# Relational messages on two row halves of the array, and the edge network's stores on ScalarE's DMA queue with a third input buffer

## The chip, the cores and the metric

The kernel runs on one core of a Trainium2 chip. The metric is the device time of one execution in microseconds. Before the change three timed executions took 13,983.0, 14,011.58 and 14,035.43 us, a median of 14,011.58. Engines are named as in the profile: PE does matrix multiplications (PEld its weight loads), DVE is VectorE, ACT is ScalarE, POOL is GpSimd, SP is SyncE, which here only issues DMAs.

## The reference

A graph with 3125 nodes of 64 features goes through four layers, each ahead of a layer norm and a relu. 100,000 edges, sorted by target, carry attributes of 32, 64 and 9 numbers and one of 65 relation types. Cut to the two places that the change touches:

```python
# layer 1 (tensor field): weights of every edge from its 64 attributes, once for k, once for v
def mlp2(x, w1, b1, w2, b2):
    return jax.nn.relu(x @ w1 + b1) @ w2 + b2
wk = mlp2(edge_features, k_w1, k_b1, k_w2, k_b2)      # [E, 128]
wv = mlp2(edge_features, v_w1, v_b1, v_w2, v_b2)      # [E, 128]
k = tensor_product(x_dst, edge_sh, wk, Cqk)           # sh: 9 numbers of every edge
v = tensor_product(x_dst, edge_sh, wv, Cv)

# layer 3 (relational convolution), twice: W_r is [65, 64, 64]
seg = dst * r + edge_type
msg = x[src]
agg = segment_sum(msg, seg).reshape(n, r, d)
cnt = segment_sum(ones, seg).reshape(n, r, 1)
mean = agg / maximum(cnt, 1.0)
out = einsum('nrd,rdk->nk', mean, W_r) + x @ W_root + b
# around it
conv = relu(out)
res = relu(h @ res_W[l] + res_b[l])
h = conv + res
```

Layer 0 is three transformer convolutions (attention over the incoming edges of a node), layer 2 two mean convolutions.

## The kernel before

The stages run one after the other: sorting the edges by target, three transformer loops, the tensor field's loop, two mean convolutions, two relational convolutions. Each loop goes over the edges in 49 groups; a group has 16 slots of 128 edges, and for every slot POOL issues one indirect DMA (`gather`, L56) that fetches 128 rows of a node table by index. Plain DMAs go through the helper `dma` (L53), which issues all of them on SP's queue, in the order in which SP reaches them: an instruction of SP that waits holds back all behind it. The engines each work through their own instructions in order; which order that is is decided by a scheduler at build time, apart from the few instructions marked `keep_in_program_order`.

*Relational convolution* (`rgcn`). The kernel multiplies first and gathers afterwards: for each of 25 blocks of 125 nodes it computes the product of the block with all 65 relation matrices, 125 x 4160 numbers, and stores them in the DRAM table `xw` (`store_nodes`). `edge_sum` then gathers one 64-wide row for each edge by source and relation. `hT` holds the transposed features (64 partitions; `transposed`, L340 and L341, over a PSUM tile `ptr` in two buffers), `wr` the 65 matrices side by side on the same 64 partitions. One block is one matmul for root and residual weights (L924, `po`, 128 columns), with two additions of biases on DVE (L925 and L926), and nine matmuls L931 into the PSUM tile `pm` (three buffers of one bank): eight of 512 columns (eight relations), and one of 64. Each `pm` is copied to `xs` (three buffers), by DVE (L936) and ACT (L934) in turn. Contraction runs over 64 partitions, so the matmuls use rows 0 to 63 of the array. In the profile every float32 matmul appears as two weight loads and two matmul records.

*Edge network* (`edge_weights`). A generator with 98 steps, each for eight slots of 128 edges, that the transformer loops draw on: two half steps in each third group, one half step in the other groups, so two steps to every three groups. A step loads `ef` (the 64 edge features and the nine harmonics, two buffers), transposes it over `pe` and `eT`, multiplies by the first weights (L565, the halves of the array in turn) with a relu on ACT into `hid` (L566), then splits the harmonics into three bf16 parts (L571 to L575) and transposes them into `sT` (L580), which two DMAs store in `sht`. Last it multiplies by the second weights (biases L588, products L594, PSUM tiles `pw`), and ACT copies the result into `wo` (L597); a DMA of 1024 KB stores it in `wt`. A further DMA writes zeros to `qxf`. ACT also does the transformer's own exponentials (L418, `ew`) in the same queue; DVE's L423 needs them and gives buffers free for later gathers.

Of the kernel before, what the change touches and what calls it, by code (L numbers as in the profile page):

```python
# [8 lines left out]
F32 = mybir.dt.float32  # L9
# [8 lines left out]
P = 128  # L18
N = 3125
NP = 125  # L20
NT = 25
D = 64
# [10 lines left out]
DE, DS, DF = 32, 9, 64  # L33
# [3 lines left out]
R = 65  # L37
# [4 lines left out]
def gnn_stack(ctx: ExitStack, tc: tile.TileContext, a: dict, out: bass.AP):  # L42
    nc = tc.nc
    V, S, PE, GP = nc.vector, nc.scalar, nc.tensor, nc.gpsimd
# [7 lines left out]
    def dma(dst, src):  # L52
        return nc.sync.dma_start(dst, src)  # L53
# [51 lines left out]
    wt = dram.tile([EP, 2 * OV], F32, name="wt")  # L105
# [4 lines left out]
    with tc.tile_pool(name="skey", bufs=1) as kp, tc.tile_pool(name="swork", bufs=2) as wp, tc.tile_pool(  # L110
        name="srow", bufs=3
# [11 lines left out]
        for name, pad in (("dst", N), ("src", 0), ("edge_type_65", 0)):  # L123
            t = kp.tile([P, NG, G], I32, name=f"k_{name}")
# [30 lines left out]
        for g in range(NG):  # L155
            oh = one_hots(g)
            for j in range(G):
                PE.matmul(ph, lhsT=oh[:, j, :HI], rhs=oh[:, j, HI:], start=(g == 0 and j == 0),
                          stop=(g == NG - 1 and j == G - 1))
# [4 lines left out]
        po = pp.tile([HI, 2], F32, name="po", tag="ph")  # L164
# [11 lines left out]
        for g in range(NG):  # L176
# [21 lines left out]
            for j in range(G):  # L198
                for s0, s1 in ((0, G // 2), (G // 2, G)):
                    s0 = max(s0, j)  # L200
# [320 lines left out]
    def edge_weights(cp, ep, pp):  # L521

        w1 = cp.tile([P, P], F32, name="w1")
        b1 = cp.tile([P, 1], F32, name="b1")
        w2 = cp.tile([P, OV], F32, name="w2")
        b2 = cp.tile([3, 2, OV], F32, name="b2")
        for i, nm in enumerate(("k", "v")):
            for k in range(2):
                dma(w1[k * D:(k + 1) * D, i * D:(i + 1) * D], a[f"L1_gnn_{nm}_w1"])
            dma(b1[i * D:(i + 1) * D, :], a[f"L1_gnn_{nm}_b1"].rearrange("(d o) -> d o", o=1))  # L530
            dma(w2[i * D:(i + 1) * D, :], a[f"L1_gnn_{nm}_w2"])
            dma(b2[:, i, :], bcast_rows(a[f"L1_gnn_{nm}_b2"], 3))

        parts = [cp.tile([3, 2, OV], BF16, name=f"b2p{k}") for k in range(3)]
        acc = cp.tile([3, 2, OV], F32, name="b2acc")
        for k, t in enumerate(parts):
            V.tensor_copy(t, b2)
            if k < 2:
                V.tensor_sub(b2, b2, t)
        V.tensor_scalar(acc, parts[0], ident[:3, 0:1], None, op0=ALU.mult)  # L540
        for k in (1, 2):
            V.scalar_tensor_tensor(acc, parts[k], ident[:3, k:k + 1], acc, op0=ALU.mult, op1=ALU.add)
        b2r = cp.tile([3, 2, OV], BF16, name="b2r")
        V.tensor_copy(b2r, acc)
        one3 = cp.tile([3, P], BF16, name="one3")
        V.memset(one3, 1.0)
        zeros = cp.tile([P, 8, OV], F32, name="zeros")
        V.memset(zeros, 0.0)
        rows = sht.rearrange("t k p -> (t k) p")
        for s0 in range(0, NS, 8):  # L550
            ef = ep.tile([P, 8, DF + DS], F32, name="ef")
            dma(ef, tab.rearrange("(p j) f -> p j f", p=P)[:, s0:s0 + 8, C64:C64 + DF + DS])
            pe = pp.tile([P, 4, P], F32, name="pe", tag="pe", bufs=2)
            for i in range(4):
                e2 = ep.tile([P, 2, DF], F32, name="e2")
                c = S.copy(e2, ef[:, 2 * i:2 * i + 2, :DF])
                if i == 0:
                    tc.keep_in_program_order(c)
                PE.transpose(pe[:, i, :], e2.rearrange("p a f -> p (a f)"), ident)
            eT = ep.tile([P, 4, P], F32, name="eT")  # L560
            S.copy(eT, pe)
            hid = ep.tile([P, 2, 4, P], F32, name="hid")
            for k in range(2):
                ph = pp.tile([P, 4, P], F32, name="ph", tag="pe", bufs=2)
                PE.matmul(ph, lhsT=w1[k * D:(k + 1) * D, :], rhs=eT[k * D:(k + 1) * D], start=True, stop=True)  # L565
                S.activation(hid[:, k], ph, AF.Relu, bias=b1)  # L566
            yield
            sh = ef[:, :, DF:]
            s3 = ep.tile([P, 8, 3, DS], BF16, name="s3")
            rest = ep.tile([P, 2, 8, DS], F32, name="srest")  # L570
            tc.keep_in_program_order(S.copy(s3[:, :, 0, :], sh))  # L571
            V.tensor_sub(rest[:, 0], sh, s3[:, :, 0, :])
            S.copy(s3[:, :, 1, :], rest[:, 0])
            V.tensor_sub(rest[:, 1], rest[:, 0], s3[:, :, 1, :])
            S.copy(s3[:, :, 2, :], rest[:, 1])  # L575
            pst = pp.tile([4 * 3 * DS, 2, P], BF16, name="pst", tag="pe", bufs=2)
            for q in range(2):
                PE.transpose(pst[:, q, :], s3[:, 4 * q:4 * q + 4].rearrange("p j k s -> p (j k s)"), identb)
            sT = ep.tile([4 * 3 * DS, 2, P], BF16, name="sT")
            S.copy(sT, pst)  # L580
            for q in range(2):
                t0 = (s0 + 4 * q) * 3 * DS
                dma(rows[t0:t0 + 4 * 3 * DS, :], sT[:, q, :])
            wo = ep.tile([P, 8, 2 * OV], F32, name="wo")
            for i0 in (0, 2):
                pw = [pp.tile([P, 2, 2, OV], F32, name=f"pw{m}") for m in range(2)]
                for m in range(2):
                    PE.matmul(pw[m], lhsT=one3, rhs=b2r[:, m, :].unsqueeze(1).to_broadcast([3, 4, OV]),  # L588
                              start=True, stop=False)
                for i in range(2):  # L590
                    for k in range(2):
                        for m in range(2):
                            r = slice(m * D, (m + 1) * D)
                            PE.matmul(pw[m][:, i, k, :], lhsT=hid[r, k, i0 + i, :], rhs=w2[r, :], start=False,  # L594
                                      stop=(i == 1 and k == 1))
                for m in range(2):
                    S.copy(wo[:, 2 * i0:2 * i0 + 4, m * OV:(m + 1) * OV], pw[m].rearrange("p i k o -> p (i k) o"))  # L597
            dma(wt.rearrange("(p j) f -> p j f", p=P)[:, s0:s0 + 8, :], wo)
            dma(qxf[0:EP, :].rearrange("(p j) f -> p j f", p=P)[:, s0:s0 + 8, :], zeros)
            yield  # L600

# [305 lines left out]
    def rgcn(l):  # L907
        xw = dram.tile([N, R * D], F32, name=f"xw{l}")
        with tc.tile_pool(name="rg", bufs=1) as fp, tc.tile_pool(name="rgp", bufs=2, space=PSUM) as pp:
            own = fp.tile([NP, NT, D], F32, name="own")  # L910
            res = fp.tile([NP, NT, D], F32, name="res")
            with tc.tile_pool(name="rw", bufs=1) as rp:
                wr = rp.tile([D, R, D], F32, name="wr")
                dma(wr, a["L3_gnn_W"][l].rearrange("r d k -> d r k"))
                wo = rp.tile([D, 2 * D], F32, name="wo")
                dma(wo[:, :D], a["L3_gnn_root"][l])
                dma(wo[:, D:], a["L3_gnn_res_W"][l])
                bb = rp.tile([NP, 2 * D], F32, name="bb")
                dma(bb[:, :D], bcast_rows(a["L3_gnn_bias"][l], NP))
                dma(bb[:, D:], bcast_rows(a["L3_gnn_res_b"][l], NP))  # L920
                hT = transposed(rp, pp, h, D, "hT")
                for t in range(NT):
                    ps = pp.tile([NP, 2 * D], F32, name="po", tag="pn")
                    PE.matmul(ps, lhsT=hT[:, t, :], rhs=wo, start=True, stop=True)  # L924
                    V.tensor_add(own[:, t, :], ps[:, :D], bb[:, :D])  # L925
                    V.tensor_add(res[:, t, :], ps[:, D:], bb[:, D:])  # L926
                    xs = rp.tile([NP, R * D], F32, name="xs", bufs=3)
                    for k, r0 in enumerate(range(0, R, 8)):
                        n = min(8, R - r0) * D
                        pm = pp.tile([NP, 8 * D], F32, name="pm", bufs=3)  # L930
                        PE.matmul(pm[:, :n], lhsT=hT[:, t, :], rhs=wr[:, r0:r0 + n // D, :].rearrange("d r k -> d (r k)"),  # L931
                                  start=True, stop=True)
                        if k % 2:
                            S.copy(xs[:, r0 * D:r0 * D + n], pm[:, :n])  # L934
                        else:
                            V.tensor_copy(xs[:, r0 * D:r0 * D + n], pm[:, :n])  # L936
                    store_nodes(nodes(xw[:])[:, t, :], xs)
                V.tensor_scalar(res, res, 0.0, None, op0=ALU.max)
            agg = edge_sum(fp, xw.rearrange("n (r k) -> (n r) k", r=R), msgi, f"r{l}", weight=wrel)
            V.tensor_add(own, own, agg)  # L940
            V.scalar_tensor_tensor(h, own, 0.0, res, op0=ALU.max, op1=ALU.add)
# [37 lines left out]
```

## Time and profile before

The profiled execution took 13,998.9 us, its span on the core 13,997.1 us.

| what | us |
|---|---|
| timed, median of 3 | 14,011.58 |
| profiled execution | 13,998.9 |
| its span | 13,997.1 |
| sort, 0 to 1420 | 1420 |
| transformer loops (three) | 1222, 1210, 1243 |
| tensor field loop, 5730 to 8310 | 2580 |
| mean convolutions' gathers (two) | 1098, 1094 |
| relational products (two) | 347, 344 |
| relational gathers (two) | 1113, 1217 |
| busy over the span: PE, DVE, ACT, POOL | 5371.2, 6166.8, 1256.5, 8020.8 |

The stage bounds are read from where the instructions of one stage end and those of the next begin. The page gives busy times over the whole span; since the stages have different limits, a share of the span says little, and a stage has to be read by itself. In a line of a group the numbers after the bar are busy time in us, mean ns of one, then the idle time of the engine just before these instructions and what ended it. "Remote" as a releaser means another core or a queue that the profile could not place; the kernel has only one core.

### The profile page before, as it was taken

How to read it: one execution, taken by the hardware profiler on the slowest of the kernel's cores; microseconds unless marked ns; L12 is line 12 of the kernel's file. 1: busy time of each engine (PE TensorE's matmuls, PEld its weight loads, DVE VectorE, ACT ScalarE, POOL GpSimd, SP SyncE). 2: the span in 40 equal slices, each digit the busy share in tenths (PEclk: the TensorE clock that was granted, in tenths of full speed). 3: DMA queues.
4: the chain of work that ended last, by engine and by line, in shares of the span. 5: the costliest groups of instructions: out<-in, count | busy, mean ns of one | idle time of the engine just before them, and what ended most of it. 6: DMA issues, size and time to landing. Idle time of an engine off the chain costs nothing. (4 is left out here: it accounts for less than half of the span.)

```text
span 13997.1 us, 80542 instructions
## 1 busy us (share of the span) xinstructions
PE 5371.2 (38%) x21850; PEld 3428.6 (24%) x21850; DVE 6166.8 (44%) x16155; ACT 1256.5 (9%) x3433; POOL 8020.8 (57%) x7569
## 2 busy tenths in 40 slices
PE   4444344434443443588888860000000900045000
PEld 4333122222222222366666640000000400022000
DVE  6444355535553555366666654443442222222222
ACT  0000122212221221000000000000000100000000
POOL 4666466666666666433333325777777067633776
PEclk7666555555555555799999985555555555555555
DMA  5443755434443443223332221111111421133111
GB/s 165 104 109 92 119 174 183 157 88 140 133 124 95 135 133 113 84 106 110 110 110 106 104 72 38 47 48 40 45 46 45 135 60 45 45 93 101 47 45 42
DMA packets 1290163, 1325.60 MB, mean 95 GB/s; under 512 B 1042585, under 2 KB 1044579, under 8 KB 1245581
## 3 DMA queue, kind: packets, MB, share of 16 engines
q1 hardware_dynamic: 1037387, 948.58, 22.5%
q0 software_dynamic: 252320, 371.88, 10.1%
q8 instruction: 172, 2.82, 0.1%
q14 instruction: 284, 2.33, 0.1%
HBM read 727.92 MB, written 591.40 MB: 94 GB/s over the span
## 5 line engine op out<-in xcount | busy, mean ns | idle before, releaser
L56 POOL DMA_INDIRECT kvg<-kvt,srci x2352 | 2428.2, 1032 | 1192.8 <-issue 679.3
L56 POOL DMA_INDIRECT msg<-xw,msgi x1568 | 1587.9, 1013 | 1342.1 <-issue 515.0
L501 DVE SCALAR_TENSOR_TENSOR msg<-msg,same 128x64 f32<-128x64 f32 x3132 | 905.6, 289 | 2615.0 <-DVE msg L501 1095.2
L56 POOL DMA_INDIRECT msg<-ht,srci x1568 | 1661.8, 1060 | 618.5 <-issue 472.6
L56 POOL DMA_INDIRECT xg<-xtf,srci x784 | 916.8, 1169 | 1512.8 <-PE px L801 1287.8
L814 PE MATMUL pa<-cc,zT 128*128 128x256 f32 x6272 | 1623.4, 415 | 65.3 <-DVE zT L809 65.3
L506 PE MATMUL pv<-msg,prevm 128*128 128x64 f32 x8 | 2.7, 440 | 3926.3 <-DVE msg L501 3926.3
L814 PEld LDWEIGHTS pa<-cc,zT 128*128 128x128 f32 x6272 | 1254.9, 206 | 630.6 <-issue 231.2
L231 POOL DMA_INDIRECT tab<-rows,posi x784 | 817.7, 1043 | 597.1 <-issue 369.9
L368 DVE SCALAR_TENSOR_TENSOR data<-data,same 128x66 f32<-128x66 f32 (+2 forms) x3136 | 938.5, 299 | 98.7 <-DVE qg L368 59.2
L506 PEld LDWEIGHTS pv<-msg,prevm 128*128 128x128 f32 x8 | 2.0, 311 | 3927.0 <-issue 2246.6
L368 DVE SCALAR_TENSOR_TENSOR qg<-qg,same 128x64 f32<-128x64 f32 (+1 forms) x2940 | 867.9, 295 | 107.9 <-DVE data L368 49.3
L652 PE MATMUL pe<-we,eaT 128*128 128x256 f32 x1176 | 587.9, 638 | 413.1 <-DVE kvg L654 239.9
L588 PE MATMUL pw<-b2r,one 3*128 3x512 bf16 x392 | 199.2, 526 | 1207.7 <-ACT wo L597 807.2
L931 PE MATMUL pm<-wr,hT 64*125 64x512 f32 x900 | 645.7, 910 | 0.7 <-DVE xs L936 0.7
L809 DVE TENSOR_TENSOR zT<-xT,pb 128x512 f32<-128x512 f32 x980 | 632.3, 678 | 25.3 <-issue 23.8
L822 DVE TENSOR_TENSOR kvg<-kvg,pa 128x512 f32<-128x512 f32 x392 | 255.7, 684 | 873.2 <-PE pa L818 836.0
L594 PE MATMUL pw<-w,hid 64*128 64x128 f32 x3136 | 440.1, 371 | 208.9 <-ACT hid L566 110.1
L594 PEld LDWEIGHTS pw<-w,hid 64*128 64x128 f32 x3136 | 347.5, 248 | 557.5 <-issue 369.6
L652 PEld LDWEIGHTS pe<-we,eaT 128*128 128x128 f32 x1176 | 330.2, 319 | 588.3 <-DVE kvg L654 263.1
L654 DVE TENSOR_TENSOR kvg<-kvg,pe 128x1024 f32<-128x1024 f32 x294 | 358.9, 1221 | 251.0 <-DMA kvg<-kvt,srci 181.5
L216 PE MATMUL pb<-free,oht 49*128 49x64 f32 x1566 | 290.5, 364 | 379.3 <-ACT oht L213 253.6
(297 smaller groups left out, 8346.5 us busy)
## 6 DMA issues: line engine op xcount, KB each, us to landing
wt<-wo SPq DMA_DIRECT2D x98, 1024.0 KB
kvg<-wt SPq DMA_DIRECT2D x49, 2048.0 KB
xw<-xs SPq DMA_DIRECT2D x50, 1820.0 KB
qg<-qx SPq DMA_DIRECT2D x144, 512.0 KB
cum_tf<-data SPq DMA_DIRECT2D x49, 1152.0 KB
cum_t<-data SPq DMA_DIRECT2D x98, 544.0 KB
qxf<-zeros SPq DMA_DIRECT2D x98, 512.0 KB
cum_s<-msg SPq DMA_DIRECT2D x98, 512.0 KB
```

Of the source, the lines that this page charges most:

```text
L56: return GP.indirect_dma_start(out=dst, out_offset=None, in_=table, in_offset=bass.IndirectOffsetOnAxis(ap=idx, axis=0),)
L216: PE.matmul(pb[:, j, :], lhsT=oht[:, j, :], rhs=free[:, j - 1, :] if j else base, start=True, stop=True)
L231: st = GP.indirect_dma_start(out=tab[:], out_offset=bass.IndirectOffsetOnAxis(ap=posi[:, g, j:j + 1], axis=0), in_=rows[:, j, :], in_offse ...
L368: V.scalar_tensor_tensor(t[:, j], t[:, j - 1], same[:, s:s + 1], t[:, j], op0=ALU.mult, op1=ALU.add)
L501: V.scalar_tensor_tensor(m[:, j, :], prev, same[:, g * G + j:g * G + j + 1], m[:, j, :], op0=ALU.mult, op1=ALU.add)
L594: PE.matmul(pw[m][:, i, k, :], lhsT=hid[r, k, i0 + i, :], rhs=w2[r, :], start=False, stop=(i == 1 and k == 1))
L652: PE.matmul(pe[:, i], lhsT=eaT[:, 2 * b + i, :], rhs=we, start=True, stop=True)
L654: V.tensor_add(kve, kve, pe.rearrange("p i j d -> p (i j) d").unsqueeze(2).to_broadcast([P, 8, 2, D]))
L809: V.tensor_mul(z, xT, pb)
L814: PE.matmul(pa[i // 2][:, i % 2, :], lhsT=zT[c][:, i, :], rhs=cc[:, c, :], start=(c == 0 and i % 2 == 0), stop=False)
L822: V.tensor_mul(kv, kv, pa[i2])
L931: PE.matmul(pm[:, :n], lhsT=hT[:, t, :], rhs=wr[:, r0:r0 + n // D, :].rearrange("d r k -> d (r k)"), start=True, stop=True)
```

## The change

Two places change. In `rgcn`, the 65 relation matrices are split: 33 lie on partitions 0 to 63 and 32 on partitions 64 to 127 of `wr` (two loads), the root and residual weights on partitions 64 to 127 of `wo`. The features are copied twice side by side into `hh` (one copy by DVE, one by ACT), so that their transposition puts the same `hT` on both halves of the partitions; `ptr` has one buffer. In a block, matmuls of the lower and the upper half follow each other, four pairs of 512 columns, then the 64-column matmul on the lower half and the 128-column one for `po` on the upper half. DVE copies the lower half's results, ACT those of the upper half and the 64 columns. `pm` has five buffers, `po` one. The number of matmul columns, the copies to `xs` and the stores to `xw` are as before.

In `edge_weights`, the two stores of `sT` and the store of `wo` are issued on ACT's DMA queue, and `ef` has three buffers. The loads and the zeros of `qxf` stay on SP's queue. In the order built, SP has 294 DMA issues less over the kernel and ACT 294 more, and the scheduler also places some PE and DVE instructions of the transformer loops otherwise than before.

```diff
--- before.py
+++ after.py
@@ -548,7 +548,7 @@
         V.memset(zeros, 0.0)
         rows = sht.rearrange("t k p -> (t k) p")
         for s0 in range(0, NS, 8):
-            ef = ep.tile([P, 8, DF + DS], F32, name="ef")
+            ef = ep.tile([P, 8, DF + DS], F32, name="ef", bufs=3)
             dma(ef, tab.rearrange("(p j) f -> p j f", p=P)[:, s0:s0 + 8, C64:C64 + DF + DS])
             pe = pp.tile([P, 4, P], F32, name="pe", tag="pe", bufs=2)
             for i in range(4):
@@ -580,7 +580,7 @@
             S.copy(sT, pst)
             for q in range(2):
                 t0 = (s0 + 4 * q) * 3 * DS
-                dma(rows[t0:t0 + 4 * 3 * DS, :], sT[:, q, :])
+                S.dma_start(rows[t0:t0 + 4 * 3 * DS, :], sT[:, q, :])
             wo = ep.tile([P, 8, 2 * OV], F32, name="wo")
             for i0 in (0, 2):
                 pw = [pp.tile([P, 2, 2, OV], F32, name=f"pw{m}") for m in range(2)]
@@ -595,7 +595,7 @@
                                       stop=(i == 1 and k == 1))
                 for m in range(2):
                     S.copy(wo[:, 2 * i0:2 * i0 + 4, m * OV:(m + 1) * OV], pw[m].rearrange("p i k o -> p (i k) o"))
-            dma(wt.rearrange("(p j) f -> p j f", p=P)[:, s0:s0 + 8, :], wo)
+            S.dma_start(wt.rearrange("(p j) f -> p j f", p=P)[:, s0:s0 + 8, :], wo)
             dma(qxf[0:EP, :].rearrange("(p j) f -> p j f", p=P)[:, s0:s0 + 8, :], zeros)
             yield
 
@@ -910,30 +910,39 @@
             own = fp.tile([NP, NT, D], F32, name="own")
             res = fp.tile([NP, NT, D], F32, name="res")
             with tc.tile_pool(name="rw", bufs=1) as rp:
-                wr = rp.tile([D, R, D], F32, name="wr")
-                dma(wr, a["L3_gnn_W"][l].rearrange("r d k -> d r k"))
-                wo = rp.tile([D, 2 * D], F32, name="wo")
-                dma(wo[:, :D], a["L3_gnn_root"][l])
-                dma(wo[:, D:], a["L3_gnn_res_W"][l])
+
+                R0 = (R + 1) // 2
+                halves = (slice(0, D), slice(D, 2 * D))
+                wr = rp.tile([2 * D, R0, D], F32, name="wr")
+                wo = rp.tile([2 * D, 2 * D], F32, name="wo")
+                for k, r0, r1 in ((0, 0, R0), (1, R0, R)):
+                    dma(wr[halves[k], :r1 - r0, :], a["L3_gnn_W"][l][r0:r1].rearrange("r d k -> d r k"))
+                dma(wo[D:, :D], a["L3_gnn_root"][l])
+                dma(wo[D:, D:], a["L3_gnn_res_W"][l])
                 bb = rp.tile([NP, 2 * D], F32, name="bb")
                 dma(bb[:, :D], bcast_rows(a["L3_gnn_bias"][l], NP))
                 dma(bb[:, D:], bcast_rows(a["L3_gnn_res_b"][l], NP))
-                hT = transposed(rp, pp, h, D, "hT")
+                hh = rp.tile([NP, NT, 2, D], F32, name="hh")
+                V.tensor_copy(hh[:, :, 0, :], h)
+                S.copy(hh[:, :, 1, :], h)
+                hT = transposed(rp, pp, hh.rearrange("p t k d -> p t (k d)"), 2 * D, "hT", bufs=1)
                 for t in range(NT):
-                    ps = pp.tile([NP, 2 * D], F32, name="po", tag="pn")
-                    PE.matmul(ps, lhsT=hT[:, t, :], rhs=wo, start=True, stop=True)
+                    xs = rp.tile([NP, R * D], F32, name="xs", bufs=3)
+                    for i in range(4):
+                        for k in range(2):
+                            pm = pp.tile([NP, 8 * D], F32, name="pm", bufs=5)
+                            PE.matmul(pm, lhsT=hT[halves[k], t, :],
+                                      rhs=wr[halves[k], 8 * i:8 * i + 8, :].rearrange("d r k -> d (r k)"),
+                                      start=True, stop=True)
+                            c0 = (k * R0 + 8 * i) * D
+                            (S.copy if k else V.tensor_copy)(xs[:, c0:c0 + 8 * D], pm)
+                    pm = pp.tile([NP, 8 * D], F32, name="pm", bufs=5)
+                    PE.matmul(pm[:, :D], lhsT=hT[halves[0], t, :], rhs=wr[:D, R0 - 1, :], start=True, stop=True)
+                    ps = pp.tile([NP, 2 * D], F32, name="po", tag="pn", bufs=1)
+                    PE.matmul(ps, lhsT=hT[halves[1], t, :], rhs=wo[D:, :], start=True, stop=True)
+                    S.copy(xs[:, (R0 - 1) * D:R0 * D], pm[:, :D])
                     V.tensor_add(own[:, t, :], ps[:, :D], bb[:, :D])
                     V.tensor_add(res[:, t, :], ps[:, D:], bb[:, D:])
-                    xs = rp.tile([NP, R * D], F32, name="xs", bufs=3)
-                    for k, r0 in enumerate(range(0, R, 8)):
-                        n = min(8, R - r0) * D
-                        pm = pp.tile([NP, 8 * D], F32, name="pm", bufs=3)
-                        PE.matmul(pm[:, :n], lhsT=hT[:, t, :], rhs=wr[:, r0:r0 + n // D, :].rearrange("d r k -> d (r k)"),
-                                  start=True, stop=True)
-                        if k % 2:
-                            S.copy(xs[:, r0 * D:r0 * D + n], pm[:, :n])
-                        else:
-                            V.tensor_copy(xs[:, r0 * D:r0 * D + n], pm[:, :n])
                     store_nodes(nodes(xw[:])[:, t, :], xs)
                 V.tensor_scalar(res, res, 0.0, None, op0=ALU.max)
             agg = edge_sum(fp, xw.rearrange("n (r k) -> (n r) k", r=R), msgi, f"r{l}", weight=wrel)
```

## The prediction

> **What bounds the kernel now.** I read the page first for shares (PE 38%, DVE 44%, POOL 57%: no engine bounds the whole), then the windows table by stage, then the chain and the waits inside the two kinds of stage that the change touches. Columns of the windows table: stretch, length, busy time with count of PE, PEld, DVE, ACT and POOL, granted clock, DMA share, GB/s.
>
> ```profile
> 1568.00:2790.00 1222.00, 520.75 (x2062) 306.13 (x2062) 645.18 (x2073) 251.47 (x771) 810.39 (x784) 0.59 0.56 171
> 2960.00:4170.00 1210.00, 521.51 (x2044) 305.56 (x2044) 640.16 (x2056) 249.44 (x768) 801.75 (x774) 0.58 0.45 132
> 4330.00:5573.00 1243.00, 523.07 (x2014) 305.80 (x2014) 647.80 (x2070) 242.28 (x755) 805.97 (x784) 0.57 0.44 129
> ...
> 10890.00:11237.00 347.00, 334.90 (x505) 140.59 (x503) 83.84 (x175) 60.01 (x103) 0.12 (x1) 0.55 0.46 150
> ...
> 12436.00:12780.00 344.00, 337.65 (x525) 142.41 (x525) 84.27 (x177) 62.18 (x107) 0.00 (x0) 0.55 0.45 148
> ```
>
> The last two rows are the message matmuls of the two relational layers: PE is busy for 97%, DVE, ACT and POOL hardly, the DMA engines under half. PE alone is the bound. The chain in the first of them (start, length, what) shows the price of one block of 125 nodes, nine matmuls of two records each:
>
> ```profile
> 10906.43 7.03 PE pm L931 x18
> ...
> 10928.72 14.07 PE pm L931 x18
> ...
> 10951.77 274.59 PE pm L931 x350
> ...
> 11227.35 8.28 DMA xw<-xs
> ```
>
> 7.03 us at full clock, 14.07 at half, and the clock is half from 10930 on. Everybody waits for PE (waits of the same stretch; engine, who for whom, sum, times, longest):
>
> ```profile
> ACT xs L934 <- PE pm L931: 275.6, 100, 9.7
> DVE xs L936 <- PE pm L931: 240.1, 120, 2.7
> ```
>
> The three transformer loops (first three rows) hold the edge network, so the queue edits act there. POOL's gathers are the fullest engine. From the page, and from the waits over the three loops:
>
> ```profile
> L56 POOL DMA_INDIRECT kvg<-kvt,srci x2352 | 2428.2, 1032 | 1192.8 <-issue 679.3
> ```
> ```profile
> ACT wo L597 <- remote: 1096.1, 91, 33.6
> PE pw L588 <- ACT wo L597: 806.7, 150, 33.7
> DVE data L423 <- ACT ew L418: 716.0, 39, 27.1
> ...
> POOL kvg L56 <- DVE qg L368: 343.3, 39, 14.9
> ```
> ```profile
> SPq L53 <- remote: 559.1, 26, 57.4
> SPq L53 <- ACT sT L580: 402.3, 59, 34.9
> ```
>
> Of POOL's 1192.8 us idle, 679.3 is its own issuing; 513.5 us is waiting. That is the most that the queue edits could win, over three loops. A stall comes back about every 73 us (three groups of 16 gathers): ACT stands before its copy L597, DVE then lacks the exponentials of L418 queued behind it, and after some 25 us POOL runs out of free kvg buffers. SP stands for ACT's sT with loads behind it.
>
> **What the Trainium skill says.** "TensorEngine Tiling (Array Packing)", When to Use Tiling: a contraction of at most 64 allows two row tiles; PSUM Bottleneck: evacuation isn't sped up, so share it between ScalarE and VectorE. The trace of before agrees that two halves run together: the edge network's L565 already alternates halves, and its pair of 512-column matmuls (four records) took 2.08 us at half clock in the timeline at 1969.57, where two of L931 take 3.4. "TensorE: Matmul & The Clock Gate", Part 1: the clock is full or half, by activity. The trace agrees on two values (1.00, 0.50), but a PE that was 97% busy fell to half. "DMA: Bandwidth & Descriptors", Issuing engines are not separate DMA queues: issuing from another engine only saves issue time. The trace can't show the other case; all large transfers here come from SP.
>
> **The change part by part.**
>
> *Message matmuls.* Per block, eight 512-column matmuls in a row become four pairs, relations 0 to 32 on rows 0 to 63 and 33 to 64 on rows 64 to 127; the 64-column matmul pairs with the 128-column one of po. At half clock one 128-column matmul takes 0.60 us (the chain has po x4, two matmuls, at 1.20), I take the same for the 64-column one, and so a 512-column one takes (14.07 - 0.60) / 8 = 1.68 us. A block is then 4 x 1.68 + 0.60 = 7.3 us, against some 14.7 with po. 25 blocks: 183 us. At full clock 3.7 us.
>
> What is late next: the xw store, 52.09 MB for 25 blocks or 2.08 MB each. At full clock before, the windows of 10 us had 304 GB/s at a DMA share of 0.93: 6.84 us a block, 171 us a layer (6.4 and 159 if the share rises to 1.0). Evictions stay under both: DVE 4 x 0.692 + 0.224 + 0.215 = 3.2 us, ACT 4 x 0.586 + 0.26 = 2.6 us a block. Five pm buffers against three let a pair wait in PSUM while the next runs.
>
> Before, from the first pm at 10891.2 to the last store's end at 11235.6 is 344.4 us. After, PE-bound at half clock: 183 + 9 for the last eviction, issue (0.31) and landing (8.28) = 192. Store-bound: 171 + 7 for the first block + 2 = 180. Added ahead of the loop: hh on DVE and ACT side by side (the 125x1600 pass L938 took 1.0 us; ACT at its 0.586 for 512 columns 1.8), and ptr on one PSUM buffer, so that transposes and the copy (0.57) alternate: seven rounds by about 0.5 us. Together 5 us. wr is two loads in place of one, issued ahead of the layernorm's end, so hidden; uncovered it would cost the order of 1 us. Layer: 185 to 197, a gain of 147 to 159; with full clock and share 1.0, 4 + 159 + 5 = 168, a gain of 176. I take 153, twice 306 us. The following gathers wait for the last store only and shift as a whole.
>
> *Stores to ACT's queue.* SP loses 98 wt and 196 sht issues, ACT gains 294. An issue on SP takes 0.325 us (wt), so ACT gets about 96 us on top of some 743 busy in 3675: covered by idle time unless an issue has to wait. What moves off SP is its standing for ACT sT (402 us), with ea, qg and ef loads and cum_t stores behind. But the waits list shows DVE short of a load almost nowhere, so early loads win little. The third ef buffer lets the ef load go one block earlier; "SPq <- ACT e" is 282 us over the loops, again not POOL's wait. In the compiled order L597 still stands ahead of L418 on ACT. So if what holds L597 isn't SP, the stall stays. "Remote" names a queue that the profile can't place, and in its place the timeline has PE standing as well (26.32 us by "issue" ahead of L588 at 2516.40, begun when L594's last matmul was recorded done). I lean to PE, which the edit doesn't touch.
>
> New waits: an issue on ACT can stand until an earlier transfer has landed, as SP's do now; behind it stand L418 and the PSUM evictions, and for these DVE L423 and PE L588 wait. Bounds over the three loops: a gain of at most 513 us, since POOL has no more; a loss of up to 559, if SP's remote waits move to ACT whole. I take a gain of 60, about 1.2 us per 73 us cycle, for early loads less the issues.
>
> *Sum.* 13,998.9 (span 13,997.1 and 1.8 around it) - 306 - 60 = 13,633. The profiled execution is 12.7 us under the median 14,011.6, 0.09%, which I leave out: 13,630.
>
> **Rivals.**
> B, *SP's order is the stall.* For: 1096 us of L597 under "remote", 402 us of SP before sT, both in the same stretches. Against: DVE waits for no load. If two thirds of the 513 go, 350: 13,999 - 306 - 350 = 13,343.
> C, *halves don't overlap* for 125-column weights. Against: L565. 13,999 + 10 - 60 = 13,949, no change.
> D, *stores as bound, slower than priced*: 16 KB rows at 150 GB/s, the average in this stage, would be 347 us a layer and no gain; against it the 304 GB/s actually seen. It is in C's share.
> E, *ACT blocked at its stores*, the slower side. Place: the wt and sht issues ahead of L418. Price: SP's 559 us of remote waits move to ACT, and POOL, already short of buffers, loses as much: 13,999 - 306 + 559 = 14,252. It decides once each of 98 blocks costs POOL over 306 / 98 = 3.1 us. Against: L597 already waits there, and a wait behind a longer one is free.
> F, *the same, mildly*: 0 to 200 lost, 13,700 to 13,890.
>
> **How the numbers follow.** Forecast 0.62 (13,480 to 13,750), B 0.20 (13,180 to 13,480), F 0.06, C and D 0.06, E 0.06. 13,630 is the likeliest. From 13,280 to 13,760 leaves out C, D, E, most of F and a tail of B, 0.2 in all. A run of this kernel tells 0.5% (70 us) from no change. Faster: forecast, B and F but its end, 0.90; same: C and a little of F, 0.05; slower: E and a little, 0.05.
>
> **What would show it.** In the relational stages: 180 to 197 us in place of 344 to 347, PE records of both halves that overlap, DMA share 0.85 or more, and DVE and ACT either waiting for PE (half clock) or xs waiting for its store. In the transformer loops: POOL's waiting near 450 and "ACT wo L597 <- remote" still near 1000, each loop within 40 us of before. Wrong it would be if a relational stage keeps over 250 us, if a loop falls under 1130 (B), or if ACT's queue shows long waits at DMA issues and DVE L423 waits over 1000 us (E).

## The result, and the profile after

The changed kernel takes 13,935.69 us (median of 6 runs, 13,913.84 to 13,955.82) beside 13,994.74 for the kernel before in the same runs: a ratio of 0.9953, 95% interval 0.9937 to 0.997. That is a gain of 59 us where 366 were forecast. The profiled execution's span is 13,911.9 us, 85.2 less than before.

The stages show two large changes of opposite sign. From the windows by stage of the changed kernel (columns as before):

```profile
1573.00:2850.00 1277.00, 521.50 (x2053) 312.08 (x2055) 651.85 (x2054) 251.40 (x766) 783.67 (x784) 0.57 0.52 164
3017.00:4299.00 1282.00, 516.67 (x2046) 306.51 (x2046) 643.62 (x2053) 251.03 (x765) 784.17 (x784) 0.57 0.44 125
4468.00:5757.00 1289.00, 515.14 (x2014) 311.96 (x2014) 655.80 (x2073) 243.79 (x755) 788.74 (x784) 0.56 0.43 124
...
11074.00:11284.00 210.00, 139.04 (x507) 78.14 (x505) 74.12 (x151) 61.12 (x128) 0.56 (x1) 0.80 0.79 248
12504.00:12702.00 198.00, 131.63 (x488) 75.55 (x484) 72.75 (x149) 58.62 (x123) 0.81 (x1) 0.81 0.83 263
```

The relational stages gave most of what was forecast: PE's busy time there fell from 335 us to under 140, the clock rose from 0.55 to 0.80, the DMA share from 0.46 to about 0.8. From the first message matmul to the first gather it was 345.8 us in the first layer (10,891.1 to 11,236.9), it is 215.2 (11,068.2 to 11,283.4); the forecast for a layer was 185 to 197. The chain there now runs through the stores:

```profile
11196.20 20.75 DMA xw<-xs
...
11217.68 2.30 PE pm L934 x5
...
11222.57 15.16 DMA xw<-xs
...
11241.56 20.65 DMA xw<-xs
```

A transfer of 15 to 21 us (up to three blocks stand in its queue, since `xs` has three buffers) is followed by a few matmuls and then by the next transfer. PE is no longer the bound.

The transformer loops got longer with the same work in them. From first to last gather they last 1252, 1257 and 1265 us, before 1197, 1199 and 1220: 158 us more. With what lies between them, the tensor field's first gathered rows reach PE at 5918.5, before at 5735.6: 183 us later. The page's line of POOL's gathers, and waits of the changed kernel over its three loops (to 5735):

```profile
L56 POOL DMA_INDIRECT kvg<-kvt,srci x2352 | 2357.0, 1002 | 1421.6 <-issue 681.1
```
```profile
ACT wo L597 <- remote: 700.8, 95, 28.7
...
POOL kvg L56 <- DVE qg L368: 549.8, 53, 18.7
...
DVE kvg L654 <- DMA kvg<-kvt,srci: 462.1, 91, 10.8
DVE kvg L654 <- PE pe L652: 376.7, 40, 26.9
```

POOL's waiting apart from its own issues rose from 513.5 to 740.5 us. ACT's standing before L597 fell by 395 us, DVE's 716 us for L418 fell to 66, and still POOL waits more: DVE now stands at L654, the addition that opens a group, for gathers and for PE.

### The profile page after: what moved, and what is told of

It reads as the page before. It is cut to its first block, busy times and chain, and to the rows that moved or that the text cites. A ratio compares the mean times of both kernels' runs of the same rounds, so it can differ in the third digit from the quotient of the medians.

```text
span 13911.9 us, 80372 instructions
## 1 busy us (share of the span) xinstructions
PE 5052.0 (36%) x21850; PEld 3367.8 (24%) x21850; DVE 6179.6 (44%) x16107; ACT 1266.6 (9%) x3485; POOL 7974.2 (57%) x7569
## 5 line engine op out<-in xcount | busy, mean ns | idle before, releaser
L56 POOL DMA_INDIRECT kvg<-kvt,srci x2352 | 2357.0, 1002 | 1421.6 <-issue 681.1
L56 POOL DMA_INDIRECT msg<-xw,msgi x1568 | 1584.8, 1011 | 1075.2 <-issue 519.4
L501 DVE SCALAR_TENSOR_TENSOR msg<-msg,same 128x64 f32<-128x64 f32 x3132 | 905.4, 289 | 2616.5 <-DVE msg L501 1065.5
L56 POOL DMA_INDIRECT msg<-ht,srci x1568 | 1660.7, 1059 | 619.3 <-issue 473.0
L56 POOL DMA_INDIRECT xg<-xtf,srci x784 | 952.2, 1215 | 1481.5 <-PE px L801 1256.6
L814 PE MATMUL pa<-cc,zT 128*128 128x256 f32 x6272 | 1690.8, 428 | 12.3 <-DVE zT L809 12.3
L814 PEld LDWEIGHTS pa<-cc,zT 128*128 128x128 f32 x6272 | 1302.1, 214 | 582.2 <-issue 208.3
L368 DVE SCALAR_TENSOR_TENSOR data<-data,same 128x66 f32<-128x66 f32 (+2 forms) x3136 | 937.4, 299 | 330.5 <-DVE qg L368 149.1
L368 DVE SCALAR_TENSOR_TENSOR qg<-qg,same 128x64 f32<-128x64 f32 (+1 forms) x2940 | 865.8, 294 | 201.3 <-DVE data L368 110.7
L654 DVE TENSOR_TENSOR kvg<-kvg,pe 128x1024 f32<-128x1024 f32 x294 | 359.0, 1221 | 944.6 <-DMA kvg<-kvt,srci 462.1
L588 PE MATMUL pw<-b2r,one 3*128 3x512 bf16 x392 | 204.5, 539 | 987.1 <-issue 509.6
L594 PE MATMUL pw<-w,hid 64*128 64x128 f32 x3136 | 457.5, 388 | 197.2 <-ACT hid L566 98.1
L594 PEld LDWEIGHTS pw<-w,hid 64*128 64x128 f32 x3136 | 362.6, 262 | 538.0 <-issue 354.3
L807 PE MATMUL pb<-sh,sel 27*128 27x512 bf16 x980 | 319.8, 389 | 233.3 <-DVE zT L809 227.0
```

Of the source, the lines that this page charges most:

```text
L56: return GP.indirect_dma_start(out=dst, out_offset=None, in_=table, in_offset=bass.IndirectOffsetOnAxis(ap=idx, axis=0),)
L368: V.scalar_tensor_tensor(t[:, j], t[:, j - 1], same[:, s:s + 1], t[:, j], op0=ALU.mult, op1=ALU.add)
L501: V.scalar_tensor_tensor(m[:, j, :], prev, same[:, g * G + j:g * G + j + 1], m[:, j, :], op0=ALU.mult, op1=ALU.add)
L654: V.tensor_add(kve, kve, pe.rearrange("p i j d -> p (i j) d").unsqueeze(2).to_broadcast([P, 8, 2, D]))
L807: PE.matmul(pb, lhsT=sel[:, c, :], rhs=sh[:, j0:j0 + 4, :], start=True, stop=True)
L814: PE.matmul(pa[i // 2][:, i % 2, :], lhsT=zT[c][:, i, :], rhs=cc[:, c, :], start=(c == 0 and i % 2 == 0), stop=False)
```

## The experiments

All ratios are against the kernel before in the same runs. Unless said otherwise a kernel holds the relational part of the change.

**One part at a time.** `e1_rgcn` takes the edge network's edits back:

```diff
-            ef = ep.tile([P, 8, DF + DS], F32, name="ef", bufs=3)
+            ef = ep.tile([P, 8, DF + DS], F32, name="ef")
...
-                S.dma_start(rows[t0:t0 + 4 * 3 * DS, :], sT[:, q, :])
+                dma(rows[t0:t0 + 4 * 3 * DS, :], sT[:, q, :])
...
-            S.dma_start(wt.rearrange("(p j) f -> p j f", p=P)[:, s0:s0 + 8, :], wo)
+            dma(wt.rearrange("(p j) f -> p j f", p=P)[:, s0:s0 + 8, :], wo)
```

`e3_rgcn_act` takes back only the first of the three, `e4_rgcn_wt` the first two, `e5_rgcn_sht` the first and the third.

> Only the relational part of the change; the edge network's DMAs all on SP's queue and two ef buffers, as before. If the relational stages of the changed kernel are what the part is worth by itself, they give back about 269 us in all, and the three transformer loops stay at 1197, 1199 and 1220 us from first to last gather: 13,725 to 13,740. If the two parts depend on each other (other PE or DMA state left behind), the loops lengthen here too, and the time stays near 13,930.

> The relational part and all three stores on ScalarE's queue, but two ef buffers. If the stores are what lengthens the loops, the time is that of the changed kernel, 13,930, within 0.3%, and each loop lasts 1250 to 1265 us. If the third ef buffer does it, the loops are back at 1197 to 1220 and the time is 13,730.

> The relational part and the wt store alone on ScalarE's queue. In the order built, this one edit already changes most of what the stores change on PE (2515 lines of difference against 2937) and on DVE (5815 against 5894). If the order of the instructions is what lengthens the loops, this kernel has most of the loss: 13,880 to 13,940. If it is the number of DMA issues on ScalarE, it has a third of it (98 of 294): about 13,790.

> The relational part and the two sht stores alone on ScalarE's queue: 196 of the 294 issues, with little change of the order on PE and DVE (448 and 700 lines of difference against 284 and 360 of the relational part by itself). If the order does it, 13,720 to 13,750, perhaps less since SP no longer stands for sT with loads behind it; if the issues on ScalarE do it, two thirds of the loss, 13,860.

| kernel | median us | ratio | 95% interval |
|---|---|---|---|
| `e1_rgcn` | 13,730.18 | 0.9802 | 0.9782 to 0.9822 |
| `e3_rgcn_act` | 13,935.57 | 0.9941 | 0.9921 to 0.9961 |
| `e4_rgcn_wt` (wt alone on ACT) | 13,856.74 | 0.9898 | 0.9875 to 0.9921 |
| `e5_rgcn_sht` (sht alone on ACT) | 13,760.66 | 0.9821 | 0.9798 to 0.9843 |

The relational part alone is worth 269 us (13,999.51 to 13,730.18) and leaves the loops at 1200, 1186 and 1191 us. The stores on ACT give back 205 of it; the third `ef` buffer changes nothing that can be measured (`e3_rgcn_act` against the changed kernel). The 98 wt issues cost 127 us and the 196 sht issues 30, which the interval of `e1_rgcn` covers: the loss doesn't follow the number of issues. Both times lie outside the ranges stated for the order, 13,857 below 13,880 and 13,761 above 13,750, but further from those stated for the number of issues (13,790 and 13,860). Together the stores cost more (205) than the two by themselves (157).

**Order or queue.** Moving a DMA to ACT does two things: it uses another queue, and it makes the scheduler lay out PE, DVE and ACT otherwise. Two kernels separate them by edges for the order of issue (no semaphore, no wait), which hold the three engines in the loops to the order taken from another build:

```diff
+    for packed in ORDERS:
+        ...
+            tc.add_manual_dep(
+                at[name], prev,
+                mybir.DependencyInfo(mybir.DependencyClass.NoSync, mybir.DependencyReason.DATA),
+                reason="pin",
+            )
```

> The relational part and all three stores on ScalarE's queue, but PE, DVE and ACT held to the order that they have with the stores on SP's queue (edges for the order of issue alone, no waits added); the stores stand right behind the copies that feed them. If the changed order is what lengthens the loops, they are back near 1185 to 1200 us each and the time is 13,720 to 13,760. If the queue does it (issues on ACT, waits ahead of them, transfers in other company), the time stays at 13,900 to 13,940. In between, the two share it.

> The opposite: the stores on SP's queue, PE, DVE and ACT held to the order that they have with the stores on ScalarE's. If the order does it, 13,900 to 13,940; if the queue does it, 13,720 to 13,760.

| order of PE, DVE, ACT | stores on SP | stores on ACT |
|---|---|---|
| as built with stores on SP | 0.9802 (`e1_rgcn`) | 0.9845, 0.9828 to 0.9861 (`p1_act_sporder`) |
| as built with stores on ACT | 0.9925, 0.9907 to 0.9942 (`p2_sp_actorder`) | 0.9941 (`e3_rgcn_act`) |

Down a column is the order: 0.0123 and 0.0096 of 14,000, or 172 and 134 us. Along a row is the queue: 0.0043 and 0.0016, 60 and 22 us. The first of these is clear of the two intervals, but a repetition of the kernel of `e1_rgcn` further down gave 0.9819, which leaves 36; the second is within them. `p1_act_sporder` took 13,806.29 us, between its two ranges; `p2_sp_actorder`, 13,913.41, lies in the one for the order. So the order is the larger part of the loss, and the queue has a small one or none. The waits say the same. DVE's waits over the loops (to 5700) of `p2_sp_actorder`, with every store on SP, look like the changed kernel's:

```profile
DVE kvg L654 <- DMA kvg<-kvt,srci: 549.7, 102, 10.6
DVE kvg L654 <- PE pe L652: 383.1, 36, 25.6
```

and those of `p1_act_sporder`, with every store on ACT, look like those before:

```profile
DVE data L423 <- ACT ew L418: 683.2, 39, 26.0
DVE srest L572 <- ACT s L571: 335.2, 51, 32.9
DVE kvg L654 <- DMA kvg<-kvt,srci: 190.5, 62, 7.9
```

ACT never stood at a store of its queue: in the changed kernel's trace the longest gap ahead of one of its 294 issues is 0.6 us, and their own time sums to 116 us.

**Which place in the order.** DVE's order, cut to the lines that matter (first row with the stores on SP, two groups in three; second row with the stores on ACT, one group in three):

```
L414  L654  L415  L417  L654        L423  L661  16 pairs of scans
L414  L654  L415  L417  L654  L654  L423  L661  16 pairs of scans
```

L661 frees the group's `kvg`; the third L654 in the second row belongs to the group after next, whose gathers have hardly landed, and it stands ahead of L661. `e9_act_dve` (stores on ACT) forbids that:

```diff
+                    with tc.issue_after(freed[-2].ins) if len(freed) > 1 else nullcontext():
-                    V.tensor_add(kve, kve, pe.rearrange(...))
+                        V.tensor_add(kve, kve, pe.rearrange(...))
...
-                    V.tensor_mul(data[:, :, :, :C], ...)
+                    freed.append(V.tensor_mul(data[:, :, :, :C], ...))
```

> The relational part and all three stores on ScalarE's queue, with one edge for the order of issue: DVE's additions to a group's kvg (L654) come behind the product that frees the buffer of the group two before it (L661). That takes away the place in each three groups where DVE stands for gathers of the group after next with the current one unfinished. If that place is the loss through the order, DVE's wait for PE L652 ahead of L654 (383 us) goes, its wait for the gathers falls from 550 towards 230 us, and the time falls from 13,935 to what the queue by itself costs: 13,780 to 13,830. If another difference of the order does it, 13,900 or more.

It took 13,855.48 us, 0.9886 (0.9862 to 0.991): between the two, 0.0055 of the 0.0096 that the order costs on ACT's queue. The expected 13,780 to 13,830 was missed. The place itself did go: in the traces 133 of the 294 additions of the loops stand ahead of the L661 of the group two before in `e3_rgcn_act`, and none in `e1_rgcn` or here, and DVE's idle time ahead of the additions fell from 927 to 361 us (287 in `e1_rgcn`). But POOL's wait for buffers, "POOL kvg L56 <- DVE qg L368", stayed at 531 us (556 in `e3_rgcn_act`, 341 in `e1_rgcn`). So this place is not the whole loss. Much of DVE's and ACT's order shifted elsewhere with this edge, so the figure isn't that of the one place alone either, and which other places cost the rest isn't shown.

**What ACT waits for.** In the kernel before, the timeline around one stall (start, length, engine, line; in brackets the idle time ahead and its releaser):

```profile
2488.02 1.65 PE L594 MATMUL pw<-w,hid 64*128 64x128 f32 x12
...
2515.76 0.59 ACT L597 COPY wo<-pw 128x512 f32<-128x512 f32 x1 [28.06 <-remote]
...
2516.40 0.58 PE L588 MATMUL pw<-b2r,one 3*128 3x512 bf16 x1 [26.32 <-issue]
```

L597 waits for PE's count and for an earlier store of `wo`. The trace's semaphore events have that store at 2483.45 and PE's count at 2515.74, 26 us after the recorded end of L594. I call this a late report of PE; the label "remote" hid it.

What it waits for isn't shown, and one reading turns the stall around. In the kernel before, 48 of the waits of L597 under "remote" are longer than 10 us; they make up 906 of the 1096 us. In 31 of the 48 POOL's gathers had already stopped when the report came, and in 21 of these the report came 3.5 to 5 us after the end of POOL's last gather. From the timeline, POOL's and ACT's lines:

```profile
2075.28 0.95 POOL L56 DMA_INDIRECT kvg<-kvt,srci  x1 [0.30 <-issue]
...
2080.78 0.59 ACT L597 COPY wo<-pw 128x512 f32<-128x512 f32 x1 [33.00 <-remote]
...
2088.90 0.95 POOL L56 DMA_INDIRECT kvg<-kvt,srci  x1 [12.67 <-DVE qg L368]
```

Either the late report makes POOL run out of buffers, or many a report comes only once the gathers pause. No run changed the gathers to tell the two apart. The label also stands elsewhere in the kernel before: in the sort, where PE's counts come late, and in the gathers of the convolutions, where DVE's L501 waits for DVE's own count, which comes up to 4.4 us after the recorded end:

```profile
DVE sel L218 <- remote: 315.0, 15, 34.1
...
DVE msg L501 <- remote: 308.6, 158, 4.4
```

Four kernels tried to get rid of the late reports in the loops or of their effect. `e8_exp` puts the exponentials ahead of the held-up copies on ACT:

```diff
-                S.activation(ew, ew, AF.Exp)
+                exps.append(S.activation(ew, ew, AF.Exp))
...
+                    with tc.issue_after(exps[-1].ins) if exps else nullcontext():
-                    S.copy(wo[:, 2 * i0:2 * i0 + 4, m * OV:(m + 1) * OV], ...)
+                        S.copy(wo[:, 2 * i0:2 * i0 + 4, m * OV:(m + 1) * OV], ...)
```

> The relational part with the stores on SP's queue, and one edge for the order of issue: the copies of wo (L597) come behind the exponentials (L418) of the group before. DVE keeps its order. If DVE's 709 us of standing for L418 behind a held-up L597 is what makes POOL run out of buffers (341 us), most of both goes: 13,350 to 13,600, below both kernels. If the hold-up only moves to PE's next L652 and from there to DVE's L654, nothing is won: 13,700 to 13,800.

It took 13,898.51 us, 0.9911 (0.9888 to 0.9935): slower by about 1% than without the edge, more than the rival had said. DVE's and POOL's waits there (in its source the lines from L418 to L594 stand two further down: L571 is L573, L556 is L558):

```profile
DVE srest L574 <- ACT s L573: 1069.9, 40, 35.6
```
```profile
POOL kvg L56 <- DVE qg L368: 643.5, 46, 21.0
```

DVE's wait for L418 fell to 191 us and ACT's "remote" wait before the copies to 522, but the late reports now meet ACT at other instructions that read PE's results. Three of these, L558 (the most), L563 and L568, stand ahead of ACT's cast L573, and DVE, which works in order, stands for the cast:

```profile
ACT e L558 <- remote: 435.3, 35, 23.6
```

The stall moved to a place where it costs more.

`e7_pw2` gives the first `pw` tile two PSUM buffers, so that L588 needn't wait for ACT; `e6_bias_f32` multiplies the biases in as one float32 row (`b2f`, loaded once):

```diff
-                pw = [pp.tile([P, 2, 2, OV], F32, name=f"pw{m}") for m in range(2)]
+                pw = [pp.tile([P, 2, 2, OV], F32, name=f"pw{m}", bufs=2 - m) for m in range(2)]
```
```diff
-                    PE.matmul(pw[m], lhsT=one3, rhs=b2r[:, m, :].unsqueeze(1).to_broadcast([3, 4, OV]),
+                    PE.matmul(pw[m], lhsT=one3, rhs=b2f[:, m, :].unsqueeze(1).to_broadcast([1, 4, OV]),
```

> The relational part with the stores on SP's queue and a second PSUM buffer for the first of the two pw tiles, so that the bias matmul L588 of the next half needn't wait for ScalarE's copy L597. DVE and ACT keep their order. If PE's wait for the copy is part of what holds up L594's completion, 'ACT wo L597 <- remote' falls well below the 1045 us of the kernel with one buffer and POOL's wait below 340: 13,550 to 13,700. If the hold-up comes from elsewhere, nothing moves: 13,730.

> As the kernel with the relational part alone, but the biases of the edge network are multiplied in as one float32 row in place of three bf16 rows. If the hold-up of ScalarE's L597 hangs on the bf16 bias matmul, whose weights are loaded ahead of a matmul that waits, it goes and the loops shorten: 13,500 to 13,700. If not, PE is busier by about 392 times 0.6 us in idle time, and the order changes: 13,700 to 13,800.

They took 13,768.75 us (0.9819, 0.9797 to 0.9841) and 13,873.32 us (0.9904, 0.9883 to 0.9924); the first is the time of the kernel without the buffer within the intervals, the second is above both of its ranges. With two `pw` buffers "ACT wo L597 <- remote" is still 924 us, with the float32 row 651 us, in another order. So the reports are late without either of the two causes that were tried.

`e10_warm` adds work that nobody reads behind each group of L594:

```diff
+                for _ in range(8):
+                    tc.keep_in_program_order(PE.matmul(warm, lhsT=identb, rhs=idle, start=True, stop=True))
```

> The relational part with the stores on SP's queue, and eight bf16 matmuls of zeros, 512 columns each, behind every group of L594 matmuls; they go to a PSUM tile that nobody reads. They ask whether PE's late reports (ScalarE stands before L597 up to 31 us after the recorded end of L594) come from PE standing still or running at half clock: if so the wait 'ACT wo L597 <- remote' falls under 500 us and the loops shorten below 1185 us each, 13,400 to 13,650. If not, PE has some 500 us more to do (1568 matmuls of about 0.3 us) in its idle time and the loops stay or grow: 13,720 to 13,900.

It ran together with `e11_ptr2` where the kernel before itself took 12,985.85 us (9 runs, 12,984 to 12,994) in place of 14,000, so only ratios compare: 0.9794 (0.9779 to 0.9809) and 0.978 (0.9766 to 0.9793). There the reports were on time in both; `e11_ptr2` leaves the edge network as in `e1_rgcn`. Its gathers on the page, and its waits over the loops:

```profile
L56 POOL DMA_INDIRECT kvg<-kvt,srci x2352 | 2440.2, 1037 | 716.8 <-issue 696.7
```
```profile
DVE kvg L654 <- DMA kvg<-kvt,srci: 1128.2, 209, 12.1
...
ACT wo L597 <- PE pw L594: 349.9, 180, 6.7
```

Nothing in the whole kernel waits under "remote". POOL waits for only 20 us beside its own issues, DVE waits for gathers, and the three loops last 1050, 1054 and 1050 us from first to last gather. This is POOL's bound, from which the prediction took its limit of 513 us on the gain. Here POOL issues its gathers almost without a pause and the reports are still on time, so gathers alone don't make them late. But the loops are not all that differs: of the 999 us between the profiled spans of `e1_rgcn` and `e11_ptr2` they have 423, the sort's gathers 229 and the relational gathers 186. Whatever made this pair of runs faster acts on more than the edge network.

Six more runs looked for this case: the kernel before, the changed one, the relational part alone, and `e10_warm` as `f_warm`, then the changed kernel twice more.

> The kernel before, with a profile in the same place as the next three. In the last pair of runs it took 12,986 us in place of 14,000, and the kernels beside it showed no late reports of PE at all (no 'ACT wo L597 <- remote'), with POOL's gathers of a group at 21.1 us. If this run is again at 12,986, its profile should show the same: loops near 1050 us, POOL waiting only for its own issues. If it is at 14,000, loops near 1200 us and some 1000 us of 'ACT wo L597 <- remote'.

> The changed kernel. If the stores' loss is the changed order meeting PE's late reports, then without late reports (before at 12,986) POOL bounds the loops whatever the order, the loss is gone and the ratio is that of the relational part, 0.978 to 0.981. If the order or the queue costs by itself, the ratio stays near 0.993 to 0.996. With late reports (before at 14,000) it is 0.9953 again.

> The relational part alone, stores on SP's queue: 0.978 to 0.981 with or without late reports.

> Eight matmuls of zeros behind each group of L594 matmuls. Without late reports 0.979 again, as in the first run. With late reports, which it hasn't met yet: if they come from PE standing still or at half clock, 'ACT wo L597 <- remote' falls under 500 us and the ratio under 0.975; if not, 0.980 to 0.990.

> The changed kernel once more, for the case in which the kernel before takes 12,986 us beside it. Then, if the loss by the stores needs the late reports, the ratio is 0.978 to 0.981 and the loops are near 1050 us; if it doesn't, 0.990 to 0.996. With the kernel before at 14,000 beside it, it repeats 0.994 and tells nothing new.

> The changed kernel a last time, for the same question: beside a kernel before of 12,986 us a ratio of 0.978 to 0.981 and loops near 1050 us if the loss by the stores needs late reports, 0.990 to 0.996 if not; beside a kernel before of 14,000 us or more it repeats 0.990 to 0.995 and the question stays open.

The case didn't come back: before took 13,992.29 in `f_before` (its loops 1205, 1190 and 1198 us), and 14,013, 14,134 and 14,008 us in the median beside the three groups. The changed kernel was at 0.994 (0.9922 to 0.9959), 0.99 (0.9872 to 0.9927) and 0.9939 (0.9919 to 0.9959), the relational part alone at 0.9819 (0.9791 to 0.9847). `f_warm`, now with late reports, was at 0.9864 (0.9836 to 0.9891) with 866 us of "remote" before the copies (1007 in `f_rgcn`, and under 500 was asked): more work for PE doesn't bring the reports on time. Whether the stores on ACT cost anything where reports are on time stays open.

**The start of a relational stage.** `e11_ptr2` also tests the transposes:

```diff
-                hT = transposed(rp, pp, hh.rearrange("p t k d -> p t (k d)"), 2 * D, "hT", bufs=1)
+                hT = transposed(rp, pp, hh.rearrange("p t k d -> p t (k d)"), 2 * D, "hT", bufs=2)
...
-                            pm = pp.tile([NP, 8 * D], F32, name="pm", bufs=5)
+                            pm = pp.tile([NP, 8 * D], F32, name="pm", bufs=4)
```

> The relational part with the stores on SP's queue, two ptr buffers and four pm buffers in place of one and five. With one ptr buffer the profile of the relational part shows 23.4 us from the first message matmul to the first store: each round of transposes waits for ScalarE's copy and a 512-column matmul of 2.07 us stands between two rounds. With two buffers three of five such matmuls leave this place: the first store 6 to 10 us sooner in each layer, 13,710 to 13,725, if nothing else changes. If the store's rate is all that counts and the start is hidden, 13,730.

The first store is issued 11.3 us after the first message matmul (10,098.4 to 10,109.7) against 19.0 in `e1_rgcn` (10,877.8 to 10,896.8; the expectation's 23.4 counted to the store's first leg in the chain), but up to the first gather it is 207.9 against 209.8 us in the first layer and 206.0 against 212.3 in the second. The start moved by 8 us and the stage by 2 and 6. The two kernels ran where the kernel before took 12,986 and 14,000 us, so a gain in time isn't shown.

## Why the prediction was wrong

- *Message matmuls, halves side by side*: right. The 18 records of a block took 7.03 us at full clock before; in `e1_rgcn` they follow each other every 3.65 us (the forecast had 3.7), and the store is the bound, as the step on "what is late next" said:

```profile
10957.74 0.33 PE L940 MATMUL pm<-wr,hT 64*125 64x64 f32 x2
10957.86 3.81 PE L934 MATMUL pm<-wr,hT 64*125 64x512 f32 x16
10961.39 0.33 PE L940 MATMUL pm<-wr,hT 64*125 64x64 f32 x2
```

- *Its size*: forecast 306 us, measured 269. Two terms were too small. The store was priced at 304 GB/s, the rate of a window of 10 us; over 190 us of stores `e1_rgcn` moves 274 GB/s at a DMA share of 0.88, so 52.09 MB take 190 us and not 171. And the 7 us to the first store, with 3.5 for the transposes, are 19.0: a message matmul of 2 us stands between the rounds of transposes on one `ptr` buffer, which the sum had priced as seven half microseconds. The rate isn't low all the time. The sum had the 64-column matmul pair with the one for `po`, but the scheduler draws `po` of all 25 blocks into the first third of the stage, where PE and DVE take turns on its one buffer (first fence) and the stores get less to do (first row of the second; the columns are those of the windows by stage):

```profile
10933.21 0.47 PE po L942 x2
10933.69 0.22 DVE own L944
10934.19 0.47 PE po L942 x2
```
```profile
10930.00:10960.00 30.00, 24.71 (x84) 12.44 (x83) 13.49 (x37) 8.05 (x17) 0.00 (x0) 0.76 0.67 217
10960.00:11080.00 120.00, 76.12 (x280) 45.34 (x276) 40.69 (x63) 37.38 (x79) 0.00 (x0) 0.83 0.95 294
```

- *Stores to ACT's queue, "I take a gain of 60"*: this step failed; it is a loss of 205 us (`e1_rgcn` against `e3_rgcn_act`). The step priced the queue. It was right that ACT doesn't stand at its issues, whose own time is 116 us (96 in the sum), but early loads brought no gain that shows: with the order held, the queue costs 22 to 60 us. And it put nothing for the order on PE and DVE, though the section on the change says that it differs; of the order it looked only at whether L597 still stands ahead of L418 on ACT, which it does. The order costs 134 to 172 us of the loss. The signs stated for the loops failed with it: POOL's waiting is 740.5 us and not near 450, "ACT wo L597 <- remote" 701 and not near 1000, and each loop is 45 to 58 us longer, where 40 was the limit.
- *Leaning to PE for "remote"*: right. It is PE's count, and no kernel that touched the edge network's buffers or queue removed it, though the sum of these waits ranges from 520 to 1150 us with the order.
- *Rival E*: its mechanism, ACT blocked at issues, didn't happen. *Rival F*, 0 to 200 us lost, was near the loss, with a chance of 0.06 and for another reason. *Rival C*'s 13,949 lies nearest to the measured time by chance: its mechanism fell, and a gain and a loss nearly cancel. *Rival D*, stores slower than priced, came true in part, with 274 GB/s and not 150.
- *Rival B*: SP's order isn't the cause of the stall, which stays with all three stores off SP (942 us of "remote" in `p1_act_sporder`). That the stall is worth as much as B took it to be did show: the loops last 1050 us where the reports are on time.

The sum by measured terms: 269 gained, 205 lost, 64 us in all; measured 59. The loss in the order is shown by the kernels with the order held; how a changed order loses time while reports come late is shown only in part.

## What to carry to other kernels

Where a scheduler lays out the program, moving a DMA to another engine's queue can change the order on every engine; compare the orders line by line, and ask of each wait that moved which buffer it keeps occupied. To price it, hold the old order with edges and change only the queue. A stall can move when it is pushed: here each of two ways to take DVE off its wait for L418 (the order with the stores on ACT, and `e8_exp`) put it before another wait that cost more, and the relational part with the stores left on SP (0.9802) beats both kernels.

## What the runs showed of the hardware

- The TensorE clock followed more than PE's busy time. With float32 matmuls on 64 rows PE was 97% busy at a mean clock of 0.55; with both halves it is busy for 66% of the stage at 0.80. The Trainium skill ("TensorE: Matmul & The Clock Gate", Part 1) has the clock set by how busy PE has been recently; by that alone these two stages would stand the other way round. What else counts isn't shown: the stages differ in the rows in use, in the pairing and in the waits.
- PE's report of finished matmuls can reach ACT 26 us after the recorded end (33 us at most in the kernel before). DVE's can be late too, there by up to 4.4 us. Such reports came in all profiled runs but one pair, where the kernel before was 7% faster and no wait of the whole kernel was of this kind. What makes them late isn't settled; many of PE's came just after the gathers had paused.
